# Message passing by one-hot matmuls: source chunks one-hot over 25 places instead of 50, two places packed into one number, and a reordered preparation

## The chip, the core and the metric

The kernel runs on one core of one Trainium2 chip. The metric is the device time of one execution in microseconds; lower is better. Engines are named as in the profile: PE (TensorE matmul) with PEld (its weight loads), DVE (VectorE), ACT (ScalarE), POOL (GpSimd) and SP (SyncE, which here only issues DMAs).

## What is computed

One layer of an edge convolution with 6250 nodes of 128 channels and 206250 edges (100000 random pairs in both directions and one loop per node), sorted by destination:

```python
h = jnp.maximum(_layernorm(x, axis=-1), 0.0)
# inside the layer, with src, dst of every edge
feat = jnp.concatenate([h[dst], h[src] - h[dst]], axis=-1)
msg = feat @ W.T + b
out = jax.ops.segment_max(msg, dst, num_segments=x.shape[0])
return x + jnp.where(jnp.isfinite(out), out, 0.0)
```

A message is a term that depends on the destination alone plus a row of a table `Bt` (6250 rows, one per source node). So the layer needs, for every destination, the maximum over its edges of the rows `Bt[src]`.

## The kernel before, in words

**Two ways to the same maximum.** The 6250 destinations are cut into 128 lanes of `LD = 49`. A source is written as place `l` of chunk `q`: 125 places, `Q = 50` chunks. For a destination and a chunk there is mostly at most one edge. This one goes the dense way: its place is found, turned into a one-hot column, and multiplied with the chunk of the table held in SBUF. A second edge in the same (destination, chunk) cell goes the sparse way: it is put on a list of its lane (`GR = 424` entries a lane, all lanes side by side), and the list is worked off row by row with indirect DMAs from `Bt` on POOL and a running maximum on DVE.

**Front (to about 145 us).** The edges of each lane are loaded (`WIN = 1792` wide), split into place (`vm`), chunk (`q16`) and destination in the lane (`dlc`). DVE compares the key with itself shifted by 1 to 41 places, PE adds the comparisons up in the PSUM tile `dup` (`shift`, L515), so that `dup` is zero for the first edge of each cell. `val` (L581) keeps `vm` for those alone. Eleven passes of masked copies (`pass_`, L615 and L616) then close up the listed entries in `pk`; spill over a lane's end is handed to the next lane through a DMA (`hand_over`, L653, into `first`). From `pk` come the indices `ridx` (L672) for the gathers. Beside the passes, and handed out to them in the lists `among` and `rest`, PE and ACT work off the list `micro`: for 25 pairs of chunks `turn` (transposes), `product` and `remainder`, which make the table and write it to DRAM by SP (L442). Also beside the passes, `turned` transposes `q16`, `dlc` and `val` into `TQ`, `TD`, `TV`, and `own_last` checks the loops. `make_sel` (L253) builds the selectors `Sel`.

**Main part (to about 750 us).** The lanes are cut into 13 tiles of 10 lanes (490 columns; the last has 8). A tile is cut into two units of 6 and 4 lanes. For a unit, `pieces` on DVE compares `TQ` with all 50 chunk numbers (`cmp_q`, four instructions, L754, into `OHQ`, 64 places per lane) and `TD` with 14 destinations (`cmp_d`, L758), and multiplies by `TV` (`mul_d`, L761). `mats` on PE then sums, for two lanes at a time, `OHQ` (the weights, 2 x 64 columns) with `OHD` (28 columns) into the PSUM tile `pv`, 14 blocks of edges each (L791): `pv[q, destination]` is the place. `square` on ACT (four instructions, L800 and L801) writes the place and its square to `Vb`. Then come 25 pairs of chunks, in each of which, for both chunks, `one_hots` makes `z = Sel.T @ Vb` (L859), ACT takes its Relu (L860), PE multiplies with two parts of the table into `ps` (L934, four matmuls), and DVE takes the maximum (L940). After each pair `more_rows` runs the sparse steps that are due: at pair k of 325 the list has to stand at `GR * (k - 2) // 310` rows, so the steps end 12 pairs before the last. A step is a min and max on DVE (`stream_step`, L152). Gathers (L82) are issued by POOL in groups of `U = 8` rows into a ring of `GB = 6` groups; group g is issued when the first step of group g - 5 has been issued. After each group SP writes its running maxima to the DRAM table `M` (L159), and the results at the ends of the runs are fetched by 49 more gathers from `M` into `R` (`get_rows`), two after each group, when they are due.

In tiles 1 and 2, ACT also counts ends of runs (L947), one instruction and its read of the accumulator after each pair. The order of everything is the order of the program on each engine; `at_pair` puts `mats`, `square`, `pieces` and the loads at given pairs, and `between` hands a piece to a pair that has two sparse steps, at the latest by a limit that falls from pair 6 to pair 11 of the unit.

**End.** The accumulated maxima are transposed, combined with `R` and with the destination's own term (L969 to L972), and written out (L974).

Of the kernel before, what the change touches and what calls it, by code (L numbers as in the profile page):

```python
# [19 lines left out]
P = 128  # L20
# [13 lines left out]
NS = 560  # L34
ST = 576
OV = 136
GR = 424
# [4 lines left out]
UL = 6  # L42
# [11 lines left out]
def gnn_kernel(tc, x, src, dst, W, b, out):  # L54
# [5 lines left out]
    KROW = 50  # L60
    GQ = 10
    NG = GR // U
    assert GR % U == 0 and NS == GR + OV and 2 * (WIN + OV) <= 1 << PB
# [24 lines left out]
    with ExitStack() as ctx:  # L88
# [13 lines left out]
        with ExitStack() as body:  # L102
# [7 lines left out]
            IQ = keep.tile([P, Q, NBLK], BF16, name="IQ")  # L110
# [5 lines left out]
            zero = keep.tile([P, 512], BF16, name="zero")  # L116
            ridx = keep.tile([P, GR], I32, name="ridx")
# [8 lines left out]
            shift_u = keep.tile([P, 1], F32, name="shift_u")  # L126
            shift_f = keep.tile([P, 1], F32, name="shift_f")
            over_ = keep.tile([P, 1], F32, name="over_")
# [10 lines left out]
            def gather_group():  # L139
                i = state["gathered"]  # L140
                state["gathered"] = i + 1
                for j in range(U):
                    k = i * U + j
                    gather(ring(i)[:, j], Bt[:, :], ridx[:, k:k + 1])

            def stream_step():
# [11 lines left out]
                if j == U - 1:  # L158
                    S_.dma_start(M_v[:, 1 + i * U:1 + i * U + U], G)  # L159

            with ExitStack() as pre:
# [47 lines left out]
                G_.affine_select(out=wrow, in_=wrow, compare_op=ALU.is_ge, fill=-2.0, base=SQ - 1,  # L209
                                 pattern=[[0, L + 1]], channel_multiplier=-1)  # L210
                G_.memset(wmask, 0.0)
                for step_, base in ((1, 0), (1, SQ)):
                    G_.affine_select(out=wmask, in_=wmask, compare_op=ALU.not_equal, fill=1.0, base=base,
                                     pattern=[[step_, Q]], channel_multiplier=-1)
# [13 lines left out]
                G_.memset(shift_u, float(L - MID))  # L228
                G_.memset(shift_f, L - MID + 0.5)
# [18 lines left out]
                for v in Vb:  # L248
                    V.memset(v, 0.0)
                    V.memset(v[32:64], 1.0)  # L250
# [72 lines left out]
                V.tensor_scalar_mul(negb, identb, -1.0)  # L323
                for r in range(2):
                    S_.dma_start(Bp[L:L + 1, r].bitcast(F32), at(frow, r * C, [list(frow.ap[0]), [0, Q], [1, C]]))
                S_.dma_start(M_v[:, 0], none)
                V.tensor_copy(IQ, row[:, 0, :Q].rearrange("p (q o) -> p q o", o=1).to_broadcast([P, Q, NBLK]))
# [103 lines left out]
                def remainder(k):  # L431
# [6 lines left out]
                    if o + 2 == GQ:  # L438
# [140 lines left out]
                keep_on(6)  # L579
                make_sel(30, 40)  # L580
                V.scalar_tensor_tensor(val, dup, 0.0, vm, op0=ALU.is_equal, op1=ALU.mult)  # L581
# [60 lines left out]
                for h in range(4):  # L642
                    rest[3 + h].append(lambda h=h: turned(q16, TQ, h))
                    rest[4 + h].append(lambda h=h: turned(dlc, TD, h))
                    rest[5 + h].append(lambda h=h: turned(val, TV, h))
                for i, j in ((6, 0), (7, 1), (8, 2), (8, 3)):
                    rest[i].append(lambda j=j: own_last(j))
                rest[8].append(lambda: A_.activation(junk[1], less, AF.Copy, accum_out=badc[:, 0:1]))
                for i in (7, 8, 9, 10):
                    rest[i].append(lambda: tick(8))  # L650
                def hand_over():
                    for p0, p1 in ((1, 113), (113, P)):
                        S_.dma_start(first[p0:p1], pk[p0 - 1:p1 - 1, GR:GR + OV])  # L653
# [11 lines left out]
                part = pk[:, :GR]  # L665
                V.tensor_scalar(lane_dl, tail_, DB, None, op0=ALU.logical_shift_right)
# [16 lines left out]
                make_sel(40, Q)  # L683
# [35 lines left out]
                V.memset(mend_i, 0)  # L719
# [4 lines left out]
            with ExitStack() as main:  # L724
# [12 lines left out]
                units = [(l0 + h, min(UL, l0 + nl - l0 - h)) for l0, nl in tiles for h in range(0, nl, UL)]  # L737
# [312 lines left out]
```

## Time and profile before

| | |
|---|---|
| time, median of 3 runs | 784.61 us (783.87 to 787.49) |
| the profiled execution | 782.91 us, of which its span is 781.1 us |
| mean granted TensorE clock | 0.948 |
| busy: PE, DVE | 646.3 us (83%), 718.3 us (92%) |
| busy: ACT, POOL | 484.0 us (62%), 491.7 us (63%) |

A row of a group in the profile reads: line, engine, operation, written tile <- read tiles, shapes (partitions x elements), count, then busy time in us and the mean duration of one in ns, then the idle time of the engine ahead of them and what ended it. A row of the timeline reads: start, duration (both us), engine, line, operation, count, and in brackets the idle time before it and what ended that. Durations on one engine overlap a little, since the next instruction starts before the last has drained. A view by stretches gives for each stretch the busy time of every engine and in brackets its number of instructions.

### The profile page before, as it was taken

The numbers are of one execution on the slowest core, as the hardware profiler recorded it, in microseconds if no ns is written. First come the engines' busy times: TensorE is split into PE (matmuls) and PEld (weight loads), VectorE is DVE, ScalarE is ACT, GpSimd is POOL, SyncE is SP. The second block draws the span as 40 slices with busy tenths as digits, with TensorE's granted clock in tenths as the row PEclk, the third lists the DMA queues.
The fourth block names the chain that finished last, engine by engine and source line by source line (L and its number), as shares of the span: only waits on it lengthen the run. The fifth ranks groups of instructions, "written<-read, shape, count | busy, mean of one in ns | idle before, by whom it ended". The sixth has DMA issues, their size and how long they took to land.

```text
span 781.1 us, 11909 instructions
## 1 busy us (share of the span) xinstructions
PE 646.3 (83%) x3623; PEld 464.5 (59%) x3630; DVE 718.3 (92%) x1290; ACT 484.0 (62%) x1035; POOL 491.7 (63%) x521
## 2 busy tenths in 40 slices
PE   0799867679898997989899898989998897887771
PEld 0455435467566765766666666667675565665660
DVE  6999899889999999899999999999998998887884
ACT  3655467336799997576666667575765556456430
POOL 4000000577777777777777777777777777777763
PEclk9999989869999998899999999999999999999995
DMA  6532144331533433343333434343343333333395
GB/s 194 132 99 75 25 100 108 106 91 52 145 107 104 117 105 92 108 114 105 105 97 97 114 105 115 105 118 105 102 115 92 105 103 96 100 105 108 98 235 183
DMA packets 83838, 85.50 MB, mean 109 GB/s; under 512 B 9954, under 2 KB 71640, under 8 KB 83512
## 3 DMA queue, kind: packets, MB, share of 16 engines
q1 hardware_dynamic: 67027, 47.62, 21.7%
q0 software_dynamic: 16176, 36.13, 17.0%
q10 hardware_dynamic: 564, 0.92, 0.4%
q8 instruction: 30, 0.49, 0.3%
q14 instruction: 41, 0.34, 0.1%
HBM read 46.96 MB, written 40.73 MB: 112 GB/s over the span
## 4 chain that ended last, share of the span: by engine, by line
DVE 26%; PE 16%; issue 14%; DMA 13%; ACT 6%; POOL 3%; POOLq 0%; DVEq 0%
DVE acc L940 16%; DMA X<-Bt,ridx 10%; PE ps L934 9%; DVE X L152 6%; PE z L859 4%; ACT oh L860 3%; DMA R<-M,last_e 3%; PE pv L791 3%; ACT counted L947 2%; POOL R L82 2%; DVE OHQ L754 1%; POOL X L82 1%; DVE acc L938 1%; DVE OHD L758 1%; DVE OHD L761 1%
## 5 line engine op out<-in xcount | busy, mean ns | idle before, releaser
L82 POOL DMA_INDIRECT X<-Bt,ridx x424 | 429.9, 1014 | 148.4 <-issue 42.0
L860 ACT ACTIVATE oh<-z 126x490 fp32r<-126x490 f32 (+1 forms) x650 | 338.3, 580 | 179.4 <-PE z L859 178.0
L934 PE MATMUL ps<-oh,Bp 126*128 126x490 f32 (+1 forms) x1300 | 396.9, 428 | 49.6 <-DVE acc L940 48.9
L940 DVE TENSOR_TENSOR acc<-acc,ps 128x980 f32<-128x980 f32 (+1 forms) x312 | 359.1, 1151 | 13.4 <-PE ps L934 11.6
L934 PEld LDWEIGHTS ps<-oh,Bp 126*128 126x128 f32 x1300 | 241.9, 195 | 150.0 <-DVE acc L940 104.0
L859 PE MATMUL z<-Vb,Sel 128*126 128x490 f16 (+1 forms) x650 | 197.0, 378 | 13.9 <-ACT oh L860 11.4
L152 DVE SCALAR_TENSOR_TENSOR X<-X,slim 128x128 f32<-128x128 f32 x423 | 145.6, 344 | 20.2 <-DMA X<-Bt,ridx 11.1
L859 PEld LDWEIGHTS <-Sel 128*126 128x126 f16 x650 | 87.1, 142 | 32.5 <-issue 4.2
L791 PEld LDWEIGHTS <-OHQ 128*128 128x128 bf16 x910 | 62.4, 162 | 17.7 <-issue 16.8
L791 PE MATMUL pv<-OHD,OHQ 128*128 128x28 bf16 (+1 forms) x896 | 67.1, 228 | 4.5 <-DVE OHD L761 4.4
L429 POOL DMA_DIRECT2D XA<-in_x x5 | 4.5, 901 | 105.2 <-DMA XA<-acc 105.2
L754 DVE TENSOR_TENSOR OHQ<-T,IQ 128x1092 bf16<-128x1092 bf16 (+5 forms) x104 | 61.6, 599 | 0.0
L82 POOL DMA_INDIRECT R<-M,last_e x49 | 48.4, 988 | 18.2 <-issue 9.4
L504 PE MATMUL dup<-T,identb 128*128 128x512 bf16 (+1 forms) x164 | 39.5, 363 | 1.7 <-DVE T L515 1.1
L947 ACT ACTIVATE counted<-lane_dl,nbias 128x560 bf16<-128x560 int32 x50 | 40.8, 815 | 0.1
L421 PE MATMUL pm<-wT,hT 128*125 128x256 f32 x100 | 30.8, 435 | 7.5 <-ACT hT L410 7.3
L421 PEld LDWEIGHTS pm<-wT,hT 128*125 128x125 f32 x100 | 19.9, 210 | 14.8 <-ACT hT L410 12.3
L504 PEld LDWEIGHTS <-identb 128*128 128x128 bf16 x168 | 16.1, 99 | 17.2 <-issue 4.5
L816 ACT COPY acc<-z 128x490 f32<-128x490 f32 (+1 forms) x13 | 7.3, 565 | 26.1 <-PE z L815 26.1
L616 DVE COPY_PREDICATED pk<-big,pk 128x1927 int32<-128x1927 int32 (+12 forms) x13 | 22.9, 1764 | 0.4
L404 ACT ACTIVATE hs<-X,nmr,rstd 125x128 f32<-125x128 f32 x50 | 22.1, 497 | 0.5 <-DVE nmr L301 0.5
L515 DVE TENSOR_TENSOR T<-KA,KB 128x1792 bf16<-128x1792 int16 x21 | 21.4, 1081 | 0.0
(255 smaller groups left out, 441.6 us busy)
## 6 DMA issues: line engine op xcount, KB each, us to landing
M<-X SPq DMA_DIRECT2D x53, 512.0 KB
X<-Bt,ridx POOLq DMA_INDIRECT x424
XA<-in_x POOLq DMA_DIRECT2D x5, 625.0 KB
ownb<-Bt SPq DMA_DIRECT2D x12, 245.0 KB
X<-in_x SPq DMA_DIRECT2D x5, 560.0 KB
Bt<-acc SPq DMA_DIRECT2D x5, 560.0 KB
XA<-acc SPq DMA_DIRECT2D x5, 560.0 KB
out_x<-R SPq DMA_DIRECT2D x10, 224.0 KB
```

Of the source, the lines that this page charges most:

```text
L82: G_.indirect_dma_start(out=o, out_offset=None, in_=table, in_offset=bass.IndirectOffsetOnAxis(ap=idx, axis=0))
L152: V.scalar_tensor_tensor(G[:, j], state["prev"], slim[:, k:k + 1], G[:, j], op0=ALU.min, op1=ALU.max)
L421: T_.matmul(pm[:L, j], hT[k % 2][:, j, :L], wT, start=False, stop=j == 1)
L504: T_.matmul(dup[:, c0:c1], w, e[:, c0:c1], start=first, stop=last)
L616: V.copy_predicated(pk[:, a:z], mask[:, a:z], pk[:, a + s:z + s])
L754: V.tensor_tensor(OHQ[:, :nl, a:z], over(TQ, z - a), iq, ALU.is_equal)
L791: T_.matmul(o, w, m, start=False, stop=True, skip_group_check=True)
L859: T_.matmul(z[:L + 1, :n], Sel[:, i + j], Vb[t % 2][:, :n], start=True, stop=True)
L860: A_.activation(oh[:, :n], z[:L + 1, :n], AF.Relu)
L934: T_.matmul(ps[:, j, :n], Bp[:, e, i + j], oh[j][:, :n], start=e == 0, stop=e == 1)
L940: V.tensor_tensor(a, a, ps[:, :, :n], ALU.max)
L947: A_.activation(counted.bitcast(BF16)[:, :NS], lane_dl, AF.Sign, scale=2.0, bias=nbias[:, c:c + 1], accum_out=ends[:, c:c + 1])
```

## The change

1. Chunk q of 25 to 49 shares a place in the one-hot with chunk q - 25. `OHQ` has 32 places a lane, of which 25 are compared (two `cmp_q` a unit instead of four), `mats` takes four lanes at a time (4 x 32 weight columns, 56 moving columns), and units are 4 and 6 lanes instead of 6 and 4. The place of an edge of an upper chunk is multiplied by 128 in the front (`upper`, `times`), so that `pv` holds lower place + 128 * upper place.
2. Per tile, `split` (two ACT instructions over the whole tile) rounds `pv / 128` to the upper place, `low` (one matmul with -128 on the diagonal) subtracts it from `pv`, and `features` (16 ACT instructions of 25 partitions, two or three lanes each) writes place and square of both halves to `Vb`. They are put at pairs 15 to 22 of the tile before; `square` was at pair 22. `mats` is put at pairs 0 and 2 of a unit instead of 2, 5 and 8.
3. In the front, `turn(k + 1)` comes ahead of `remainder(k)`. `val`, the transposes of `val`, `own_last` and `make_sel(30, 50)` come after `ridx`. Six filler matmuls ahead of `val` are gone. The second half of `hand_over` is issued by ACT, not SP. One gather from `M` into `mend` is put ahead of the first gathers, behind a memset on DVE.
4. `GR` is 420, not 424; the last group has four rows.

```diff
-NS = 560
+NS = 556
-GR = 424
+GR = 420
-UL = 6
+UL = 4
-    KROW = 50
+    KROW = 25
+    QH = Q // 2
+    HB = 32
+    DIG = 128.0
+    OFF = L - MID
...
-                micro = [f for k in range(NP_) for f in (lambda k=k: turn(k), lambda k=k: product(k),
-                                                         lambda k=k: remainder(k))]
+                micro = [lambda: turn(0)]
+                for k in range(NP_):
+                    micro.append(lambda k=k: product(k))
+                    if k + 1 < NP_:
+                        micro.append(lambda k=k: turn(k + 1))
+                    micro.append(lambda k=k: remainder(k))
...
-                keep_on(6)
-                make_sel(30, 40)
-                V.scalar_tensor_tensor(val, dup, 0.0, vm, op0=ALU.is_equal, op1=ALU.mult)
+                upper, times = junk
+                V.tensor_scalar(upper, q16, QH - 0.5, float(QH), op0=ALU.is_ge, op1=ALU.mult)
+                V.tensor_tensor(q16, q16, upper, ALU.subtract)
+                V.tensor_scalar(times, upper, (DIG - 1.0) / QH, 1.0, op0=ALU.mult, op1=ALU.add)
+                V.tensor_tensor(vm, vm, times, ALU.mult)
...
-                    rest[3 + h].append(lambda h=h: turned(q16, TQ, h))
-                    rest[4 + h].append(lambda h=h: turned(dlc, TD, h))
-                    rest[5 + h].append(lambda h=h: turned(val, TV, h))
-                for i, j in ((6, 0), (7, 1), (8, 2), (8, 3)):
-                    rest[i].append(lambda j=j: own_last(j))
-                rest[8].append(lambda: A_.activation(junk[1], less, AF.Copy, accum_out=badc[:, 0:1]))
+                    rest[6 + h].append(lambda h=h: turned(q16, TQ, h))
+                    rest[7 + h].append(lambda h=h: turned(dlc, TD, h))
...
-                    for p0, p1 in ((1, 113), (113, P)):
-                        S_.dma_start(first[p0:p1], pk[p0 - 1:p1 - 1, GR:GR + OV])
+                    for e, p0, p1 in ((S_, 1, 113), (A_, 113, P)):
+                        e.dma_start(first[p0:p1], pk[p0 - 1:p1 - 1, GR:GR + OV])
...
+                V.memset(mend_i, 0)
+                gather(mend, M[:P, :], mend_i[:, 0:1])
...
-                make_sel(40, Q)
+                V.scalar_tensor_tensor(val, dup, 0.0, vm, op0=ALU.is_equal, op1=ALU.mult)
+                for h in range(4):
+                    turned(val, TV, h)
+                for j in range(4):
+                    own_last(j)
+                A_.activation(junk[1], less, AF.Copy, accum_out=badc[:, 0:1])
+                make_sel(30, Q)
...
-                    ps = [lambda a=a, z=z: cmp_q(a, z) for a, z in ((0, 13), (13, 26), (26, 38), (38, Q))]
+                    ps = [lambda a=a, z=z: cmp_q(a, z) for a, z in ((0, 13), (13, QH))]
...
+                    z = min(a + 4, nl)
+                    for i in range(NBLK):
+                        w = OHQ[:, a:z, :, i].rearrange("p l q -> p (l q)")
+                        y = z - 1 if l0 + z == P else z
+                        todo = [(pv[:(z - a) * HB, off + a:off + y, near[i]:near[i] + WN], OHD[:, a:y, :, i])]
...
+                def split(t):
+                    n = cols[t]
+                    hi = two.tile([P, TL * LD], F32, name="hi", bufs=1)[:, :n]
+                    up = digits[t] = two.tile([P, TL * LD], BF16, name="up", bufs=1)
+                    A_.activation(hi, pvs[t][:, :n], AF.Identity, scale=1.0 / DIG, bias=magic[:, :1])
+                    A_.activation(up[:, :n], hi, AF.Identity, bias=magic[:, 1:])
+
+                def low(t):
+                    n = cols[t]
+                    T_.matmul(pvs[t][:, :n], ndig, digits[t][:, :n], start=False, stop=True, skip_group_check=True)
+
+                def features(t, h, j):
+                    n = cols[t]
+                    nl = n // LD
+                    src_ = (pvs[t], digits[t])[h][:, :n].rearrange("q (l d) -> q l d", d=LD)[HB * j:HB * j + QH, j:nl:4]
+                    v = Vb[t % 2][:, :n].rearrange("q (l d) -> q l d", d=LD)
+                    for k0, f, more in ((h * HB, AF.Copy, {}), (P // 2 + h * HB, AF.Square, {"bias": shift_f[HB * j:HB * j + QH]})):
+                        A_.activation(v[k0:k0 + QH, j:nl:4], src_, f, **more)
...
-                        for j, i in enumerate((2, 5, 8)):
-                            at_pair(p, i, lambda u_=p + 2, j=j: mats(u_, 2 * j, 2 * j + 2))
+                        for j, i in enumerate((0, 2)):
+                            at_pair(p, i, lambda u_=p + 2, j=j: mats(u_, 4 * j))
                         if p % 2:
-                            at_pair(p, 10, lambda t=(p + 2) // 2: square(t))
+                            t_ = (p + 2) // 2
+                            at_pair(p, 3, lambda t=t_: split(t))
+                            at_pair(p, 4, lambda t=t_: low(t))
+                            for k in range(8):
+                                at_pair(p, 4 + k - k // 4, lambda t=t_, k=k: features(t, 1 - k // 4, k % 4))
```

More of the change, by code (lines that the diff above doesn't have):

```diff
@@ L125, in gnn_kernel @@
             lane = keep.tile([P, 1], F32, name="lane")
-            shift_u = keep.tile([P, 1], F32, name="shift_u")
             shift_f = keep.tile([P, 1], F32, name="shift_f")
+            magic = keep.tile([P, 2], F32, name="magic")
             over_ = keep.tile([P, 1], F32, name="over_")
@@ L141, in gather_group @@
                 state["gathered"] = i + 1
-                for j in range(U):
+                for j in range(min(U, GR - i * U)):
                     k = i * U + j
@@ L803, in gnn_kernel @@
+                def square(t):
+                    split(t)
+                    low(t)
+                    for h in (1, 0):
+                        for j in range(4):
+                            features(t, h, j)
                 own_b = {}
@@ L844, in gnn_kernel @@
                         f()
-                    mats(u_, 0, UL)
+                    for a in (0, 4):
+                        mats(u_, a)
                 put_own(0)
```

72 lines of the change are left out of this document (34 added, 38 removed).

## The prediction

> **What bounds the kernel now.** I read the page's first parts, then the waits, then the groups, then stretches, and at last the timeline of POOL. The page's busy shares point at DVE, with its chain of work that ended last:
>
> ```profile
> PE 646.3 (83%) x3623; PEld 464.5 (59%) x3630; DVE 718.3 (92%) x1290; ACT 484.0 (62%) x1035; POOL 491.7 (63%) x521
> DVE 26%; PE 16%; issue 14%; DMA 13%; ACT 6%; POOL 3%; POOLq 0%; DVEq 0%
> L82 POOL DMA_INDIRECT X<-Bt,ridx x424 | 429.9, 1014 | 148.4 <-issue 42.0 <-DMA X<-Bt,ridx 39.6 <-DVE acc L940 21.0
> ```
>
> POOL's 63% misleads. The 148.4 us of idle time lie in slivers: from the first gather to the last, every gap is 0.30 us, whoever is named as its end. The timeline of POOL shows it (first gather, last gather, the first and the last fetch from M behind it; then the group of the fetches ahead of it):
>
> ```profile
> 143.82 1.37 POOL L82 DMA_INDIRECT X<-Bt,ridx  x1 [19.48 <-DVE swin L679]
> ...
> 735.69 0.95 POOL L82 DMA_INDIRECT X<-Bt,ridx  x1 [0.30 <-issue]
> 736.95 0.95 POOL L82 DMA_INDIRECT R<-M,last_e  x1 [0.30 <-issue]
> ...
> 770.51 0.94 POOL L82 DMA_INDIRECT R<-M,last_e  x1 [0.30 <-issue]
> ...
> L82 POOL DMA_INDIRECT R<-M,last_e x24 | 24.5, 1019 | 7.3 <-issue 4.3 <-DMA X<-Bt,ridx 3.0
> ```
>
> Between 143.82 and 736.64 POOL issues 424 gathers, 24 fetches, one gather of mend and one plain DMA: 450 in 592.8 us, 1.317 us each, never waiting. 25 fetches follow, and 9.6 us after the last of them the span ends. So POOL's queue is one unbroken chain from the front to the end, and the time is its start, plus the count of gathers, plus what lengthens one, plus the tail.
>
> DVE is a close second. In these stretches (columns: stretch, its length, busy us and instructions of PE, PEld, DVE, ACT, POOL, then clock, DMA) it is full from 440 to 580, and ACT is full in tiles 1 and 2:
>
> ```profile
> 213.00:260.00 47.00, 43.23 (x238) 32.09 (x237) 45.43 (x77) 45.35 (x107) 36.03 (x37) 0.96 0.36 101
> 260.00:306.00 46.00, 42.12 (x241) 31.49 (x239) 44.33 (x75) 44.27 (x104) 35.34 (x36) 0.96 0.41 114
> 440.00:580.00 140.00, 128.65 (x742) 95.24 (x741) 139.89 (x234) 91.42 (x177) 108.03 (x105) 1.00 0.39 109
> 580.00:736.00 156.00, 130.93 (x686) 96.84 (x684) 133.98 (x225) 89.46 (x178) 119.40 (x121) 0.95 0.36 101
> ```
>
> The groups up to 320 us say how far DVE's steps run behind the gathers: 133 against 105, 28 rows. After 580 DVE idles (133.98 of 156): it has caught up and waits for rows.
>
> ```profile
> L82 POOL DMA_INDIRECT X<-Bt,ridx x133 | 134.4, 1011 | 59.7 <-DVE swin L679 19.5 <-DMA X<-Bt,ridx 16.1 <-issue 12.8
> L152 DVE SCALAR_TENSOR_TENSOR X<-X,slim 128x128 f32<-128x128 f32 x105 | 36.1, 344 | 0.4
> ```
>
> **The change, part by part.**
>
> *Four rows fewer.* Four gathers at 1.317: -5.3 us on POOL's chain. Their four steps on DVE (0.34 each) lie beside it. The 49 fetches stay, and the tail with them: 0.
>
> *Half the comparisons.* The 104 comparisons of OHQ become 52. On DVE that is 30.8 us, off the path, since DVE isn't the bound. But a gather that meets them is longer:
>
> ```profile
> L754 DVE TENSOR_TENSOR OHQ<-T,IQ 128x1092 bf16<-128x1092 bf16 (+5 forms) x104 | 61.6, 599 | 0.0
> L761 DVE TENSOR_TENSOR OHD<-OHD,T 128x1176 bf16<-128x1176 bf16 (+2 forms) x26 | 17.0, 652 | 0.1
> L758 DVE TENSOR_TENSOR OHD<-T,IW 128x1176 bf16<-128x1176 bf16 (+2 forms) x26 | 16.9, 651 | 0.0
> ...
> 602.03 0.35 DVE L152 SCALAR_TENSOR_TENSOR X<-X,slim 128x128 f32<-128x128 f32 x1
> 602.30 0.72 DVE L754 TENSOR_TENSOR OHQ<-T,IQ 128x1092 bf16<-128x1092 bf16 x1
> 602.30 1.53 POOL L82 DMA_INDIRECT X<-Bt,ridx  x1 [0.30 <-DMA R<-M,last_e]
> ```
>
> An undisturbed gather takes 0.94; this one, begun together with a comparison, 1.53. The gathers' excess over 0.94 from the first to the last of the 474 rows of POOL is 32.9 us; 25.0 of it falls on the 154 gathers that overlap one of these three lines. By busy time 61.6 of 95.5 us is OHQ's: 16.1 us, of which half goes: -8.1. Bounds: 0 (the gather meets another DVE instruction instead) and -12 (the disturbance falls on OHQ alone). I take -8.1, in the middle, because the rows tie it to the length of the comparison. [...]
>
> *The start of POOL's chain.* The rows of the front around the removed instructions, and at its end:
>
> ```profile
> 88.41 1.46 DVE L253 TENSOR_TENSOR Sel<-wmask,wrow 128x1260 f16<-128x1260 f16 x1
> 91.69 0.38 PE L578 MATMUL pm<-ident,listed 128*1 128x128 f32 x2 [0.61 <-ACT T L574]
> 92.58 0.48 PE L418 MATMUL pm<-brow,bsel 128*125 128x512 f32 x1
> 92.90 1.02 PE L421 MATMUL pm<-wT,hT 128*125 128x256 f32 x4
> 92.94 2.02 DVE L581 SCALAR_TENSOR_TENSOR s<-dup,vm 128x1792 bf16<-128x1792 f32 x1 [3.06 <-PE dup L484]
> 94.88 0.27 DVE L582 TENSOR_SCALAR rows<-pm 1x128 f32<-1x128 f32 x1
> 96.02 0.43 PE L409 MATMUL pt<-ident,hs 125*128 125x125 f32 x2
> 96.51 0.14 DVE L590 COPY over__97<-pm 128x1 f32<-128x1 f32 x1
> ...
> 137.85 2.12 SPq L653 DMA_DIRECT2D first<-pk  x2
> 141.92 0.32 DVE L671 COPY_PREDICATED pk<-swin,first 128x136 int32<-128x136 int32 x1 [0.65 <-DMA first<-pk]
> 142.27 0.38 DVE L672 TENSOR_SCALAR ridx<-pk 128x424 int32<-128x424 int32 x1
> ```
>
> From 88.41 DVE now spends 1.46 on Sel, waits 3.06 for the filler matmuls and spends 2.02 on val. These leave; four passes over 1792 bf16 come in. Nearest rows are 0.63 for a pass with one input and 1.09 for one with two (below), so 3.4 us, done at 91.9. L582 then waits for L578, which ends at 92.07: it moves from 94.88 to 92.15, -2.7. L590, though, also waits behind PE's queue: the product (0.48 and 1.02) and the next turn (0.43) put it near 94.6 instead of 96.51: -1.9. At the end, `first` is there 4.1 us after its issue; its second half leaves SP, where the two issues take 2.12, and the earlier turn ends the table's DMAs before it: the wait of 0.65 goes. Sum -2.6. ACT's issue of the second half waits for the last pass with some transposes of dlc behind it; nothing before ridx needs them. The new gather into mend sits in POOL's 19.48 us of idle time; if its memset came late it would cost its 0.94, and if the first gather's 1.2 us behind ridx is a cold start, it takes that away. Bounds -4 and 0.
>
> ```profile
> L466 DVE TENSOR_SCALAR dlc__175<-d 128x1792 bf16<-128x1792 int16 x1 | 0.6, 629 | 0.0
> L473 DVE TENSOR_TENSOR KA<-T 128x1792 int16<-128x1792 int16 x1 | 1.1, 1093 | 0.0
> ```
>
> *ScalarE's part of split and features.* Four instructions of 0.467 (1.87 us a tile) become two over 490 columns and 16 over 147 or 98. The trace has no such shape; the nearest:
>
> ```profile
> L800 ACT ACTIVATE Vb<-pv,shift_u 50x245 f16<-50x245 f32 (+1 forms) x26 | 12.1, 467 | 0.4
> L816 ACT COPY acc<-z 128x490 f32<-128x490 f32 (+1 forms) x13 | 7.3, 565 | 26.1 <-PE z L815 26.1
> L295 ACT ACTIVATE rstd<-mv,eps 125x10 f32<-125x10 f32 x5 | 1.5, 306 | 3.6 <-DVE mv L291 3.6
> L437 ACT CAST Bp<-pm 125x256 fp32r<-125x256 f32 x25 | 9.5, 381 | 0.0
> ```
>
> Between 306 (10 columns) and 467 (245), both with a bias from memory, a Square of 147 or 98 takes about 0.40 or 0.37; from 381 for a plain copy of 256, a Copy about 0.30 or 0.27. Eight of each are 5.3, the split 2 x 0.6, together 6.5: +4.7 us a tile. Bounds: +3.3 (all at 0.25) and +7 (all at 0.467). Outside tiles 1 and 2 ACT is at 91.42 of 140, so this is covered. In tiles 1 and 2 it isn't: two tiles, +9.4 us on DVE's steps, which wait for the pairs. The first split and features, ahead of the loop, are bare too: +4.7. There DVE's moved val and longer Sel (2.0 and 1.5) add, and shorter pieces (four comparisons, 2.1), less PE work (28 matmuls) and the front's -2.6 take off: the loop starts about 4 us later measured from the first gather.
>
> What is late next is the ring: group g can't be gathered before the steps of group g - 5 have begun and its rows are written to M, so the steps may lag 40 rows, less two for that write. The lag of 28 grows by 4 + 9.4 us and by gathers 2.4 us faster by then, less the 2.4 us (four comparisons) that DVE saves in each of tiles 0 and 3: 11.0 us or some 9 rows. 37 of 38: I charge 2 us of waiting on POOL (0 to 8).
>
> *PE.* Its matmuls of L791 fall from 70 to 42 a tile, and one `low` is added; at 128.65 busy of 140 with DVE full, PE gains air and sets nothing. The earlier place of mats leaves at least one pair behind the last piece by the list's own limits. The rest of L791's gain is 0.
>
> *Sum:* -5.3 - 8.1 - 2.6 + 2 = -14.0 on the profiled execution's 782.9, so 768.9. That execution lies 1.7 under the median of the runs shown; against 784.61 it is 770.6.
>
> **The rivals.**
>
> (a) POOL never waits and the comparisons' share is the upper one: -5.3 - 12 - 3.5, about 764. For it: the lag after 580 is gone. Against: the ring's margin is one row.
>
> (b) The gathers stay at 1014 ns, since what lengthens them is not the comparison but whatever DVE runs beside it: -5.3 - 2.6 + 2 = -5.9, 778.7; if the ring costs 8 on top, no change (784). For it: gathers beside other DVE work carry 7.9 of the 32.9 us. Against it: 1.53 beside 0.94. [...]
>
> (c) Slower: ScalarE becomes the bound in pairs 15 to 22 of every tile. There it has eight pairs of Relu at 1.05, the split, 16 features and the copy of L816:
>
> ```profile
> 600.95 1.05 ACT L860 ACTIVATE oh<-z 126x490 fp32r<-126x490 f32 x2 [0.34 <-PE z L859]
> L940 DVE TENSOR_TENSOR acc<-acc,ps 128x980 f32<-128x980 f32 x132 | 153.8, 1165 | 0.0
> L938 DVE TENSOR_TENSOR acc<-ps,acc 128x980 f32<-128x980 f32 x6 | 7.0, 1170 | 0.0
> ```
>
> DVE's pair between 340 and 580 took 1.74 (240 us over 132 + 6 maxima) and would take 1.65, so eight are 13.2. ACT's are 8.4 + 6.5 + 0.57 = 15.5, and 2.3 too many; Relus run about one pair (1.7) ahead, so little is lost. With features at 0.467 and a split of 0.63 twice it is 17.7: 2.8 us lost in each of 10 tiles, and 2.2 more in tiles 1 and 2 and at the start, 35 in all. DVE has some 8 to spare: POOL needs 1.355 rows x 1.30 = 1.76 a pair and 24 fetches, so over the last 230 pairs DVE gains 25 + 31 us on its lag of 37 rows, 48 us. The end moves by 27, to 798. It decides from about 0.42 a feature. [...]
>
> **How the numbers follow.** Forecast 0.58 (own range 765 to 778), (a) 0.13, (b) 0.13, (c) 0.16. 0.5% is 3.9 us, about what a measurement of this kernel tells from no change. Faster: the forecast, (a) and 0.05 of (b): 0.76; same: the rest of (b), 0.08; slower: (c), 0.16. The range goes from 763 to 785, which leaves out most of (c) and the low end of (a).
>
> **What would show it.** In the profile after: the first gather near 141 instead of 143.82; POOL without gaps over 0.3 but for a few at groups between 300 and 400; the mean gather near 995 ns instead of 1014; OHQ x52; ACT full in tiles 1 and 2 and those tiles longer by some 5 us each; DVE with idle time in 440 to 580. It is wrong if POOL waits for DVE over long stretches, if gathers stay at 1014, or if ACT's features are 0.42 and over.

## The result, and the profile after

| | before | after |
|---|---|---|
| median | 786.08 us (6 runs) | 819.15 us (6 runs) |
| profiled execution's span | 781.1 us | 819.9 us |

The ratio is 1.041, 95% interval 1.035 to 1.046: 4% slower, against a forecast of 770.6 us and a range up to 785. The two profiled executions took 782.9 and 822.0 us, so their spans differ by 38.8 us where the medians differ by 33.1. Of the eighteen runs below, eleven fell on chips on which the kernel before took 1068 to 1103 us (medians), at a granted clock of 0.79 to 0.84 instead of about 0.95; such a run is called set aside, and no verdict rests on its time.

The groups of the changed kernel that answer to those quoted before:

```profile
L86 POOL DMA_INDIRECT X<-Bt,ridx x420 | 419.0, 998 | 156.4 <-issue 62.0 <-DVE X L158 35.4 <-DVE acc L986 17.4
L986 DVE TENSOR_TENSOR acc<-acc,ps 128x980 f32<-128x980 f32 (+1 forms) x312 | 360.3, 1155 | 74.5 <-PE ps L980 71.6 <-PE z L905 0.6
L906 ACT ACTIVATE oh<-z 126x490 fp32r<-126x490 f32 (+1 forms) x650 | 337.4, 577 | 158.9 <-PE z L905 157.1
L813 PE MATMUL pv<-OHD,OHQ 128*128 128x56 bf16 (+2 forms) x532 | 66.3, 285 | 11.8 <-DVE OHD L782 9.7 <-DMA ownb<-Bt 1.9
L775 DVE TENSOR_TENSOR OHQ<-T,IQ 128x728 bf16<-128x728 bf16 (+3 forms) x52 | 30.9, 600 | 0.0
```

The gather has come down to 998 ns (forecast 995), and DVE has lost 30.7 us of comparisons. But POOL now waits for DVE, and DVE for PE. The waits (engine and line that wait, what for, us in all, how often, the longest) of before:

```profile
DVE acc L940 <- PE ps L934: 11.6, 15, 1.6
...
PE z L859 <- ACT oh L860: 11.4, 22, 2.1
```

and of after:

```profile
DVE acc L986 <- PE ps L980: 71.6, 94, 3.5
...
PE z L905 <- ACT oh L906: 38.9, 79, 1.9
...
POOL X L86 <- DVE X L158: 35.4, 70, 6.7
```

Read from the bottom: POOL waits up to 6.7 us at a time for a sparse step, the step stands in DVE's queue behind a maximum, the maximum waits for PE's `ps`, and PE waits for ACT. By POOL's timeline the chain of gathers breaks in ten places between 269 and 465 us, 27.7 us beyond the ordinary gap of 0.30, and runs on unbroken from there. It no longer sets the time, the loop over pairs does. The chain of work that ended last, where ACT had 6% and DMA 13% before, says the same:

```profile
DVE 32%; ACT 28%; PE 24%; issue 12%; DMA 3%; POOL 1%; POOLq 0%; DVEq 0%; SPq 0%; ACTq 0%
```

The timeline of after shows the ends: first gather, first maximum (after 12.25 us of waiting), last gather, last combination of maxima.

```profile
142.12 1.06 POOL L86 DMA_INDIRECT X<-Bt,ridx  x1 [1.01 <-issue]
...
181.12 1.18 DVE L984 TENSOR_TENSOR acc<-ps,acc 128x980 f32<-128x980 f32 x1 [12.25 <-PE ps L980]
...
748.84 1.04 POOL L86 DMA_INDIRECT X<-Bt,ridx  x1 [0.31 <-DVE acc L986]
...
796.05 0.57 DVE L990 TENSOR_TENSOR acc<-acc 128x392 f32<-128x392 f32 x1
```

Before, the first maximum began at 170.48, the last gather ended at 736.64 and the last combination began at 751.64; now 46 us lie between these two, not 15. From the end of each tile's last combination (thirteen rows of L990, L944 before) come these stretches; the columns to the right are experiments that follow (`early_half` by its third run, `early_half_3`):

| us | before | after | `early_half` | `early_half_few` | `spread_front` | `b_half_cmp` |
|---|---|---|---|---|---|---|
| end of the first maximum | 171.7 | 182.3 | 180.5 | 177.6 | 177.5 | 173.7 |
| tile 0 from there | 42.9 | 46.5 | 43.4 | 42.9 | 42.9 | 41.8 |
| tiles 1 and 2 | 90.1 | 106.8 | 106.0 | 93.2 | 97.4 | 87.1 |
| tiles 3 to 8 | 266.0 | 293.4 | 283.8 | 274.3 | 281.1 | 263.5 |
| tiles 9 to 12 | 181.5 | 167.7 | 170.6 | 164.6 | 162.3 | 187.0 |
| from there to the end | 28.9 | 23.3 | 23.4 | 23.5 | 23.4 | 29.7 |
| span | 781.1 | 819.9 | 807.7 | 776.0 | 784.6 | 782.8 |

After minus before: +10.6 at the start, +3.6, +16.7 and +27.4 in tiles 0 to 8, together 58, then -13.8 where the kernel before had waited for gathers (DVE's steps 11.1 us in 11 waits), and -5.6 at the end. The stretches of after (columns as before: length, busy us of PE, PEld, DVE, ACT, POOL) for tiles 0, 1, 2 and the two long ones:

```profile
180.00:229.00 49.00, 43.09 (x201) 32.31 (x200) 38.83 (x53) 32.72 (x69) 37.73 (x39) 0.92 0.35 92
229.00:282.00 53.00, 41.96 (x197) 29.67 (x196) 41.67 (x68) 50.31 (x119) 38.68 (x39) 1.00 0.30 87
282.00:336.00 54.00, 45.68 (x205) 32.67 (x204) 42.69 (x69) 51.30 (x121) 32.79 (x34) 0.94 0.33 94
336.00:580.00 244.00, 211.78 (x996) 153.16 (x995) 212.01 (x359) 165.31 (x344) 175.97 (x178) 0.97 0.35 99
580.00:796.00 216.00, 192.99 (x927) 140.93 (x925) 195.18 (x315) 153.41 (x324) 145.18 (x147) 0.99 0.39 108
```

In tiles 1 and 2 ACT is full. From 336 on nobody is: DVE 212 of 244, PE 212, ACT 165. No engine's sum sets the time there; they take turns in waiting for each other. The ends of the maxima in DVE's timeline show where: on the mean of tiles 4 to 8 (43.5 us a tile before, 49.0 after), pairs 0 to 3 and 12 to 15, in which `mats` now stands, take 18.7 us instead of 13.6; pairs 16 to 22, with the features, 13.8 instead of 12.3; the other ten 16.5 instead of 17.6. Both places were tested.

### The profile page after: what moved, and what is told of

It reads as the page before. It is cut to its first block, busy times and chain, and to the rows that moved or that the text cites. A ratio compares the mean times of both kernels' runs of the same rounds, so it can differ in the third digit from the quotient of the medians.

```text
span 819.9 us, 11318 instructions
## 1 busy us (share of the span) xinstructions
PE 667.7 (81%) x3267; PEld 473.2 (58%) x3273; DVE 699.3 (85%) x1238; ACT 546.9 (67%) x1217; POOL 482.4 (59%) x523
## 4 chain that ended last, share of the span: by engine, by line
DVE 32%; ACT 28%; PE 24%; issue 12%; DMA 3%; POOL 1%; POOLq 0%; DVEq 0%; SPq 0%; ACTq 0%
ACT oh L906 13%; DVE acc L986 11%; PE ps L980 10%; ACT Vb L835 8%; PE pv L813 7%; PE z L905 5%; DVE X L158 4%; DVE T L531 4%; DVE pk L634 3%; ACT counted L993 2%; DVE big L633 1%; DVE stats L300 1%; ACT up L823 1%; ACT hi L822 1%; ACT acc L857 1%
## 5 line engine op out<-in xcount | busy, mean ns | idle before, releaser
L86 POOL DMA_INDIRECT X<-Bt,ridx x420 | 419.0, 998 | 156.4 <-issue 62.0
L980 PE MATMUL ps<-oh,Bp 126*128 126x490 f32 (+1 forms) x1300 | 398.1, 429 | 23.4 <-DVE acc L986 22.5
L905 PE MATMUL z<-Vb,Sel 128*126 128x490 f16 (+1 forms) x650 | 209.4, 377 | 48.4 <-ACT oh L906 38.9
L813 PE MATMUL pv<-OHD,OHQ 128*128 128x56 bf16 (+2 forms) x532 | 66.3, 285 | 11.8 <-DVE OHD L782 9.7
L813 PEld LDWEIGHTS <-OHQ 128*128 128x128 bf16 (+1 forms) x546 | 59.9, 164 | 23.2 <-issue 23.1
L86 POOL DMA_INDIRECT R<-M,last_e x49 | 47.5, 969 | 41.8 <-DMA M<-X 27.6
L993 ACT ACTIVATE counted<-lane_dl,nbias 128x556 bf16<-128x556 int32 x50 | 39.8, 796 | 0.3
L984 DVE TENSOR_TENSOR acc<-ps,acc 128x980 f32<-128x980 f32 (+1 forms) x13 | 15.1, 1163 | 21.1 <-PE ps L980 14.1
L775 DVE TENSOR_TENSOR OHQ<-T,IQ 128x728 bf16<-128x728 bf16 (+3 forms) x52 | 30.9, 600 | 0.0
L433 PE MATMUL pm<-wT,hT 128*125 128x256 f32 x100 | 28.6, 412 | 2.7 <-ACT hT L422 2.6
```

The lines of the kernel that those rows point to most:

```text
L86: G_.indirect_dma_start(out=o, out_offset=None, in_=table, in_offset=bass.IndirectOffsetOnAxis(ap=idx, axis=0))
L433: T_.matmul(pm[:L, j], hT[k % 2][:, j, :L], wT, start=False, stop=j == 1)
L813: T_.matmul(o, w, m, start=False, stop=True, skip_group_check=True)
L905: T_.matmul(z[:L + 1, :n], Sel[:, i + j], Vb[t % 2][:, :n], start=True, stop=True)
L980: T_.matmul(ps[:, j, :n], Bp[:, e, i + j], oh[j][:, :n], start=e == 0, stop=e == 1)
L993: A_.activation(counted.bitcast(BF16)[:, :NS], lane_dl, AF.Sign, scale=2.0, bias=nbias[:, c:c + 1], accum_out=ends[:, c:c + 1])
```

## The experiments

Theories: T1, the chain of gathers on POOL (the forecast's). T2, the bursts of `mats`, which stand right behind the last piece of the one-hots. T3, ACT's added instructions. T4, the front work that was moved behind the row numbers.

### Rows and comparisons, alone in the kernel before

`b_420` takes GR and NS of the change and nothing else.

```diff
-NS = 560
+NS = 556
-GR = 424
+GR = 420
```

> The kernel before, with parts of 420 rows instead of 424 and nothing else of the change (the last group of gathers and steps has four rows). All theories hold that the kernel before is bound by the chain of gathers on GpSimd, at 1.317 us a gather: 4 gathers less should give 4 to 6 us, a ratio of 0.993 to 0.995 to the kernel before. Were the pair loop on TensorE, ScalarE and VectorE as near to the bound already, as T2 and T3 make it after the change, it would be under 2 us.

782.09 us against 785.00, ratio 0.996 (0.993 to 0.999): 2.9 us (0.7 to 5.3). The 5.3 of the forecast lies at the edge of this; the direction is T1's. The mean gather of this profile is 1021 ns, with all comparisons in place, so means of single profiles differ by some ns.

`b_half_cmp` makes half the comparisons.

```diff
-ps = [... for a, z in ((0, 13), (13, 26), (26, 38), (38, Q))]
+ps = [... for a, z in ((0, 13), (13, 26))]
```

> The kernel before with the comparisons of q from 0 to 26 alone, two pieces for each unit instead of four (the other half of the one-hot stays zero, so the result lacks it); nothing else of the change. The forecast's term: a gather goes from 1014 to 995 ns, 8 us of 424 gathers, ratio 0.985 to 0.995. If the comparisons don't disturb the gathers: gathers stay at 1014 ns, ratio 0.998 to 1.002. If VectorE's saved 30 us matter beside that (T1 denies it, the loop before waited for GpSimd in its last tiles only): below 0.985.

783.19 us against 785.53, ratio 0.998 (0.994 to 1.001). Its gathers:

```profile
L82 POOL DMA_INDIRECT X<-Bt,ridx x424 | 430.3, 1015 | 147.4 <-issue 58.2 <-DMA X<-Bt,ridx 25.0 <-DVE acc L940 23.8
```

1015 ns against 1014, and 2.3 us in all (from 4.6 less to 0.5 more): the forecast's second term, -8.1 us, is not there, though a smaller one isn't excluded. Long gathers stay (by POOL's timelines between 200 and 700, 40 of 354 took over 1.2 us before, and 31 of 355 here, the longest 1.59 and 1.72 us). The excess over 0.94 us of the gathers and fetches that overlap a comparison of `OHQ` fell from 19.3 to 11.0 us, but that of all of them only from 32.9 to 32.2: nearly as much came back beside other work. Why gathers are 998 ns after the change stays open. The table shows what DVE's 30 us bought: tiles 0 to 8 are 6.6 us shorter, tiles 9 to 12 5.5 us longer. The loop ran ahead and then waited for POOL. So T1 holds for the kernel before, and of 30 us saved on DVE at most 4.6 show there.

### The bursts

`early_pieces` hands the pieces out by pair 7 instead of 11; `half_bursts` cuts each burst of 14 matmuls in two; `early_half` does both.

```diff
-for i in range(6, 12):
-    at_pair(p, i, lambda i=i: fill.update(most=11 - i))
+for i in range(3, 8):
+    at_pair(p, i, lambda i=i: fill.update(most=7 - i))
```
```diff
-for j, i in enumerate((0, 2)):
-    at_pair(p, i, lambda u_=p + 2, j=j: mats(u_, 4 * j))
+for j in range(4):   # mats(u_, first lane, first block, last block + 1)
+    at_pair(p, j, lambda u_=p + 2, j=j: mats(u_, j // 2 * 4, j % 2 * 7, j % 2 * 7 + 7))
```

> The changed kernel, with the pieces of the one-hots handed to VectorE at the latest by pairs 3 to 7 of each unit period instead of pairs 6 to 11, so that the last piece lies five pairs ahead of the matmuls that read it. T2 (the matmul bursts stand right behind the last piece, TensorE waits for it, and VectorE then waits for TensorE): the wait of L813 for OHD (9.7 us of VectorE in its worst row, and the 94 us that VectorE waits for L980) shrinks, tiles 4 to 8 go from 49 to 46 us each, and the whole to some 800 us (790 to 810). T3 (ScalarE's features are the cost): no change, 819. T1 (the gather chain on GpSimd sets the time): no change, 819. T4 (the front alone): no change.

> The changed kernel with each burst of 14 matmuls cut in two bursts of 7, at pairs 0, 1, 2 and 3 of a unit period instead of two bursts at pairs 0 and 2; the number and width of the matmuls stay. T2, in the form that it is the length of one burst that counts (1.65 us each, against 0.92 before the change): VectorE's wait for L980 behind a burst goes from up to 3.5 us to under 2, some 2 us a tile, 795 to 805 us in all. T2, in the form that the wait for the last piece counts: little change, since the first half still stands right behind that piece, 812 to 820. T3: no change, 819.

Both are set aside (1074 and 1065 us; so are `early_pieces` once more at 1077 and `early_half` twice at 1071 and 1082), so what each edit is worth alone stays open.

> The same kernel once more (pieces out by pair 7, bursts of 7 at pairs 0 to 3), because its two looks so far fell on chips that ran the kernel before in 1074 and 1081 us. On a chip that runs it in 785 us: T2 785 to 805 us with tiles 4 to 8 at 45 to 46 us; T3 815 to 820 us with tiles 4 to 8 at 49 us.

809.73 us, ratio 1.030 (1.024 to 1.036), against 1.041: about 8 us of the 33 come back, less than T2 asked. By the table it is 12.2 us of span: 1.8 at the start, 3.1 in tile 0, 0.8 in tiles 1 and 2, 9.6 in tiles 3 to 8, less 2.9 in tiles 9 to 12. In tiles 4 to 8 the pairs with bursts go from 18.7 to 16.5 us, still above the 13.6 of before. What a burst does, in the timeline of the changed kernel:

```profile
403.56 1.64 PE L813 MATMUL pv<-OHD,OHQ 128*128 128x56 bf16 x14 [1.14 <-DVE OHD L782]
...
405.51 1.05 ACT L906 ACTIVATE oh<-z 126x490 fp32r<-126x490 f32 x2 [3.08 <-PE z L905]
...
406.80 1.18 DVE L986 TENSOR_TENSOR acc<-acc,ps 128x980 f32<-128x980 f32 x1 [1.68 <-PE ps L980]
...
409.14 1.82 PE L813 MATMUL pv<-OHD,OHQ 128*64 128x28 bf16 x14
...
411.40 1.05 ACT L906 ACTIVATE oh<-z 126x490 fp32r<-126x490 f32 x2 [3.09 <-PE z L905]
...
412.45 1.18 DVE L986 TENSOR_TENSOR acc<-acc,ps 128x980 f32<-128x980 f32 x1 [1.77 <-PE ps L980]
```

PE waits 1.14 us for the last piece (L782, DVE), then holds the queue for 1.64; ACT starves 3.08 us, DVE 1.68. The second burst, with no wait ahead of it, does nearly the same. With both edits the longest wait of DVE falls from 3.5 to 2.1:

```profile
DVE acc L986 <- PE ps L980: 60.8, 100, 2.1
...
PE z L905 <- ACT oh L906: 39.0, 80, 1.9
```

PE's wait for ACT hasn't moved: that is another cause.

### What one matmul of a burst costs

`burst_kinds` gives the tiles four kinds of bursts.

```diff
+kind = t % 4
+m_ = OHD[:, a:y, :, i]              # kind 2: y = a + 2, two lanes only
+if kind == 1:
+    m_ = zero[:, :(y - a) * WN].rearrange("p (l w) -> p l w", w=WN)
+if kind == 3:
+    w = zero[:, :w.shape[1]]
-todo = [(pv[:(z - a) * HB, ...], OHD[:, a:y, :, i])]
+todo = [(pv[:w.shape[1], ...], m_)]
```

> A look at what one matmul of a burst costs. The changed kernel, but in tiles 1, 5 and 9 the moving operand is 56 columns side by side, all zero, in tiles 2, 6 and 10 only the first two lanes' 28 columns are moved against the same 128 weight columns, and in tiles 3, 7 and 11 the weights are 128 columns side by side, all zero (the one-hots' products are left out there); tiles 0, 4, 8 and 12 are unchanged. Unchanged: 0.118 us a matmul. If the number of matmuls sets the cost, as the prediction has it, all four kinds take 0.118. If the columns moved set it, tiles 2, 6 and 10 return to the 0.066 to 0.074 us of before; if their stride of 28 bytes does, tiles 1, 5 and 9 fall below 0.09; if the stride of the weights does, tiles 3, 7 and 11 do.

Its one execution took 803.20 us. The groups, with shapes apart (weights as partitions*columns, then moving partitions x columns; busy us over count is the cost of one in a burst):

```profile
L823 PE MATMUL pv<-OHD,OHQ 128*128 128x56 bf16 x98 | 11.7, 287 | 5.2 <-DVE OHD L782 5.2
L823 PE MATMUL pv<-OHD,OHQ 128*64 128x28 bf16 x84 | 10.9, 282 | 0.0
L823 PE MATMUL pv<-OHD,zero 128*128 128x56 bf16 x84 | 9.6, 281 | 1.2 <-DVE OHD L782 1.1
L823 PE MATMUL pv<-OHD,OHQ 128*128 128x28 bf16 x84 | 6.3, 228 | 1.1 <-DVE OHD L782 1.1
L823 PE MATMUL pv<-zero,OHQ 128*128 128x56 bf16 x84 | 6.2, 228 | 0.0
...
L823 PE MATMUL pv<-OHD,zero 128*64 128x28 bf16 x42 | 2.7, 231 | 0.0
```

For comparison, the kernel before by the same view:

```profile
L791 PE MATMUL pv<-OHD,OHQ 128*128 128x28 bf16 x882 | 65.3, 228 | 4.5 <-DVE OHD L761 4.4
```

0.119 us for 56 strided columns (0.114 with weights side by side), 0.074 for 56 side by side, 0.075 for 28 strided, as in the kernel before. So the columns and their stride of 28 bytes cost: if each of the 56 costs the same, an estimated 2.1 ns a column (0.119 / 56). For 28 that makes 0.060, and 0.075 was measured; what sets it there isn't shown. Two lanes alone are worse: 64 strided weight columns take 0.130, 64 side by side 0.064, while 128 strided ones show no such price (0.075 with 28 moving columns). Why 64 strided weight columns take longer than 128 isn't shown. Per tile the two kinds that the change uses make 28 x 0.119 + 14 x 0.130 = 5.15 us, against 70 x 0.074 = 5.2 before: 28 matmuls fewer, nothing saved.

`two_lanes` had two lanes a matmul (64 weight columns), in three bursts, with 8 feature instructions a tile.

```diff
-w = OHQ[:, a:z, :, i].rearrange("p l q -> p (l q)")
+w = OHQ[:, c:c + 2, :, i].rearrange("p l q -> p (l q)")   # for c in (a,), mats at pairs 0, 1, 2
```

> The changed kernel with two lanes a matmul instead of four: 28 moving columns and 64 weight columns, 70 matmuls a tile instead of 42, in bursts of 14 at pairs 0, 1 and 2; each feature instruction then covers five lanes, so there are 8 a tile instead of 16. If the four-lane matmul costs by its width (0.118 us against 0.066 us in the kernel before), TensorE does the same sum of work in shorter bursts (0.92 us against 1.65). T2: 800 to 810 us. T3: the features cost some 8 times 0.4 to 0.5, that is 3.6 us a tile instead of 5.3, a gain at the start and in tiles 1 and 2 of 4 to 5 us and a little in the others, 805 to 815. Were the number of matmuls the cost, as the prediction's 70 to 42 supposes, it would be slower than 819.

Both its runs, 1105 and 1092 us, are set aside. The second one's rows still show its weights, at a granted clock of 0.82:

```profile
L812 PE MATMUL pv<-OHD,OHQ 128*64 128x28 bf16 x882 | 117.1, 280 | 45.4 <-issue 31.5 <-DVE OHD L782 9.4 <-DVE OHQ L775 3.4
```

117.1 / 882 is 0.133 each, close to the 0.130 of `burst_kinds` and nearly twice what 128 weight columns cost there with the same 28 moving columns: the expectation, which went by the moving columns alone, was wrong.

### ScalarE's features

`few_features` leaves 12 of 16 feature instructions out of the changed kernel, `early_half_few` out of `early_half`.

```diff
-for j in range(4):            # ahead of the loop
+for j in range(1):
     features(t, h, j)
...
-for k in range(8):
+for k in (0, 4):
     at_pair(p, 4 + k - k // 4, lambda t=t_, k=k: features(t, 1 - k // 4, k % 4))
```

> The changed kernel without 12 of its 16 feature instructions a tile (only the first lane of each four gets its features, so the sums over the other lanes are left out of the result): ScalarE is relieved of some 4.0 us a tile (6 Copy of 0.27 to 0.31 and 6 Square of 0.36 to 0.40). T3 (ScalarE's added instructions are the cost): pairs 15 to 22 return to their times of before, the start is 4 us earlier, tiles 1 and 2 lose 8 us, 780 to 795 us in all. T2 (the bursts are the cost): only the start and tiles 1 and 2 gain, 805 to 812.

Both its runs, 1066 and 1064 us, are set aside.

> The kernel with early pieces and halved bursts (ratio 1.030 to the kernel before, some 810 us), without 12 of its 16 feature instructions a tile (the result lacks what they feed). T3 (ScalarE's added instructions are what is left): the first pair some 4 us earlier, tiles 1 and 2 some 5 to 8 us shorter each, pairs 15 to 24 of tiles 4 to 8 back from 20.2 to some 18 us: 775 to 788 us, ratio 0.985 to 1.005. T2 alone: only the bare start gains, 803 to 808 us, ratio 1.022 to 1.028. T1 would hold again if it came under 775 us: then the chain on GpSimd is once more what ends last.

777.66 us, ratio 0.989 (0.984 to 0.993): 32 us less than `early_half`, as T3 has it. By the table it is 2.8 at the start, 0.5 in tile 0, 12.8 in tiles 1 and 2, 9.5 in tiles 3 to 8, 6.0 in tiles 9 to 12; in tiles 4 to 8 the pairs 16 to 22 go from 13.7 to 12.5 us. The waits:

```profile
DVE acc L986 <- PE ps L980: 39.3, 64, 1.3
...
PE z L905 <- ACT oh L906: 6.2, 24, 0.9
```

PE's wait for ACT fell from 39.0 to 6.2. In the groups of the changed kernel, each of which mixes 147 and 98 columns, the features cost what was forecast (Square 0.40 or 0.37, Copy 0.30 or 0.27 us):

```profile
L835 ACT ACTIVATE Vb<-up,shift_f 25x98 f16<-25x98 bf16 (+1 forms) x52 | 20.6, 395 | 0.6
L835 ACT ACTIVATE Vb<-pv,shift_f 25x98 f16<-25x98 f32 (+1 forms) x52 | 18.5, 356 | 0.6
L835 ACT ACTIVATE Vb<-up 25x98 f16<-25x98 bf16 (+1 forms) x52 | 15.9, 305 | 1.2
L835 ACT ACTIVATE Vb<-pv 25x98 f16<-25x98 f32 (+1 forms) x52 | 13.9, 267 | 1.1
```

So their price was right. They stand close together, and right behind a burst. ACT in the changed kernel, from the split to the last features of a tile; the pairs in the middle hold two features each:

```profile
412.48 0.67 ACT L822 ACTIVATE hi<-pv,magic 128x490 f32<-128x490 f32 x1
...
416.10 1.06 ACT L906 ACTIVATE oh<-z 126x490 fp32r<-126x490 f32 x2
417.18 0.33 ACT L835 ACTIVATE Vb<-up 25x147 f16<-25x147 bf16 x1
417.52 0.42 ACT L835 ACTIVATE Vb<-up,shift_f 25x147 f16<-25x147 bf16 x1
417.96 1.05 ACT L906 ACTIVATE oh<-z 126x490 fp32r<-126x490 f32 x2
419.04 0.29 ACT L835 ACTIVATE Vb<-up 25x98 f16<-25x98 bf16 x1
419.34 0.38 ACT L835 ACTIVATE Vb<-up,shift_f 25x98 f16<-25x98 bf16 x1
419.74 1.05 ACT L906 ACTIVATE oh<-z 126x490 fp32r<-126x490 f32 x2
...
427.38 1.99 ACT L906 ACTIVATE oh<-z 126x490 fp32r<-126x490 f32 x4
```

There is no idle time in these 17 us, with 1.86 and 1.78 us from pair to pair, where the kernel before had a mean of 1.74. The four instructions of one pair (19), the split and the copy of L857 come on top. And ACT enters this stretch with nothing in stock: the row at 411.40 above, just ahead of the split, shows it starved for 3.09 us by the second burst.

### Place instead of amount, and the front

`spread_front` keeps the whole change. Features: one a pair at pairs 11 to 24. Counting: every other pair of tiles 1 to 4. Second unit's `mats`: pairs 6 to 9, pieces by pair 4, bursts halved, always 128 weight columns (two more zeroed lanes in `OHQ`). `val`, its `turned` and `own_last` are back ahead of `ridx`.

```diff
-at_pair(p, 4 + k - k // 4, lambda t=t_, k=k: features(t, 1 - k // 4, k % 4))
+at_pair(p, -1 + k * 14 // 16, lambda t=t_, k=k: features(t, 1 - k // 8, k // 2 % 4, (k % 2,)))
...
-if t in (1, 2):
+if 1 <= t <= 4 and i % 4 == 0 and c < LD + 1:
```

> The whole change with its work placed otherwise: features one instruction a pair at pairs 11 to 24 instead of four a pair at pairs 16 to 22, the fifty counting instructions at every other pair of tiles 1 to 4 instead of every pair of tiles 1 and 2, the second unit's matmuls at pairs 6 to 9 with their pieces out by pair 4, bursts halved and always 128 weight columns wide, and the added front work (val, its turning, own_last) back ahead of the row numbers as in the kernel before. If T3 is a matter of place (ScalarE is full only in pairs 16 to 22 and in tiles 1 and 2: 0.67 to 0.70 us a feature pair and 1.15 us of Relu against some 1.75 us a pair): tiles 1 and 2 at 46 to 47 us, tiles 4 to 8 at 45, the first pair near 178 us, 775 to 788 us, ratio 0.985 to 1.003. If it is their sum: 795 to 810 us, ratio 1.012 to 1.030.

788.12 us, ratio 1.002 (1.000 to 1.005): all but 2 of the 33 us are back, with every instruction of the change kept. The waits:

```profile
DVE acc L988 <- PE ps L982: 40.2, 67, 1.7
...
PE z L907 <- ACT oh L908: 24.6, 41, 1.1
```

Mostly place, then: against `early_half` this placing gives 22 us with all features there, where leaving most of them out gave 32; the other 10 stay open. It moves features, counting, bursts and front at once, so the share of the features' place alone isn't shown. And the change, placed this way, only draws level. The front's part, by the profiled executions: the first gather comes at 143.63 here, and at 140.62 to 142.12 in the four kernels above that have this work behind `ridx` (the changed kernel, `early_half_3`, `burst_kinds`, `early_half_few`); the first `z` comes at 171.40 here, and at 174.35 to 175.51 in the first three of these, which have all features. The moved work buys GpSimd some 1.5 to 3 us and costs the pair loop 3 to 4. `front_back` (that part alone) and `spread` (all but that part) were to settle T4:

> The changed kernel with only the moved front work put back as in the kernel before: val, its turning and own_last ahead of the row numbers, the turning of q16 and dlc three passes earlier, ten columns of the selection table back ahead of the sort. T4 (this work behind the row numbers delays the pair loop, which is the bound): the first pair at some 178 us instead of 182.3, the first gather perhaps 1 to 2 us later than 142.1, in all 3 to 6 us less than 819, ratio 1.033 to 1.037. If GpSimd's chain were the bound (T1): 1 to 2 us more than 819, with the first gather.

> The kernel with features and counting spread out, the second unit's matmuls at pairs 6 to 9, bursts halved and 128 weight columns wide, but the front as the change has it (so spread_front without the front's part). If the front is worth 3 to 6 us in the pair loop: 791 to 795 us, ratio 1.006 to 1.011. If the front is worth nothing once the loop is relieved: as spread_front, 788 us, ratio 1.002.

Both are set aside (1103 and 1082 us), so T4 rests on those profiles, and what it is worth in the whole stays open.

`b_front` is `b_420` with the earlier turns and the hand-over on two queues.

```diff
...
-                for p0, p1 in ((1, 113), (113, P)):
-                    S_.dma_start(first[p0:p1], pk[p0 - 1:p1 - 1, GR:GR + OV])
+                for e, p0, p1 in ((S_, 1, 113), (A_, 113, P)):
+                    e.dma_start(first[p0:p1], pk[p0 - 1:p1 - 1, GR:GR + OV])
```

> The kernel before with parts of 420 rows, each turn of the front ahead of the remainder before it, and the hand-over of the first rows on two queues. By the forecast's terms: 4 to 6 us for the rows (2.9 measured) and 2.6 us for the front (0 to 4), so 776 to 781 us, ratio 0.988 to 0.995. If the front's reordering brings nothing by itself: as with the 420 rows alone, ratio 0.996.

780.27 us against 786.15, ratio 0.991 (0.988 to 0.994): a little under 1% faster than the kernel before, and the fastest here that computes the whole result. Against the 0.996 of `b_420` the intervals just overlap, and its first gather isn't earlier in the profiled execution:

```profile
144.34 1.36 POOL L82 DMA_INDIRECT X<-Bt,ridx  x1 [23.61 <-DVE swin L683]
```

144.34 against 143.82. So what the reordering adds to the rows isn't shown.

## Why the prediction was wrong

The path was wrong: the time was summed on POOL's chain of gathers, and the loop over pairs became the path instead. The steps that let this happen are ACT's added work "covered" outside tiles 1 and 2, and PE, which "gains air and sets nothing". Term by term:

- **Four rows, -5.3:** 2.9 measured, with an interval that reaches 5.3. Right in kind.
- **Half the comparisons, -8.1:** wrong. Alone it moves the gather by 1 ns and the whole by 2.3 us (at most 4.6). One row with 1.53 beside 0.94, and a share by busy time, were read as a cause; the excess beside comparisons did fall with them, but nearly as much came back beside other work. The rival (b), under which the gathers stay, was right for the comparisons by themselves. That the gather came down to 998 ns in the whole change is, as far as this run shows, luck.
- **Start of POOL's chain, -2.6:** 143.82 to 142.12, -1.7. But the reordered turns show no gain by themselves; the work moved behind `ridx` gives it, and it comes back in the loop.
- **The loop starts 4 us later, measured from the first gather:** 12.3 later (39.0 us from the first gather to the first maximum, for 26.7). `val`, its transposes and `own_last` were costed as DVE's time alone; DVE also stands 2.8 us in one wait for PE, whose queue they fill. This and the split and features of the first tiles, which lie ahead of the loop with nothing beside them, were taken to be absorbed by the ring, because the loop wasn't thought to be the bound.
- **Tiles 1 and 2, +9.4:** 16.7 measured. ACT full was right (50.3 us busy of 53), and without most features the two tiles fall from 106.0 to 93.2. Why a full ACT costs more here than its own excess isn't shown.
- **ACT covered outside tiles 1 and 2:** this is the step that failed first. Its price was right: split and features take 6.7 us a tile, for 6.5. The overlap was wrong: without 12 of 16 features, tiles 3 to 12 are 15.5 us shorter (`early_half_few` against `early_half`). The step compared sums over a stretch (91 busy of 140). The features stand in seven pairs of 25, and there ACT takes 1.8 us and more a pair. Rival (c) named the place, but let it decide only from 0.42 us a feature, by a sum over eight pairs with a stock of one pair of Relus ahead and 8 us of spare time in DVE; at a mean of 0.33 us it decided already, and in the tile shown the burst ahead had used up the stock.
- **PE "gains air and sets nothing":** this failed too. It gained nothing, L813 66.3 us for 67.1, as the wide matmul costs 1.6 times the narrow one. And the "at least one pair behind the last piece" was not there: PE runs ahead of DVE, so it stood 1.14 us waiting for a piece that DVE had yet to make. Earlier pieces and halved bursts together are worth 8 us.
- **The ring, +2:** 27.7 us of gaps beyond the ordinary ones. The first stand in tiles 1 and 2, where the margin of one row was eaten. They followed from the late loop and didn't set the end: the last gather came 46 us before the last combination.

The sum was made on one engine's chain, and every other term was measured against whether it lengthened that chain. The loop was charged 4 + 9.4 us, which the ring was to take. It lost 58 us up to tile 8; 19 of these fell on time in which it had waited before (-13.8 and -5.6), and the rest is the 39 us by which the profiled span grew.

## What to carry to other kernels

Where two chains run within a few per cent of each other, cost a change on both, and compare an engine's load with the pace pair by pair, not by its share over a stretch: here, instructions that fit on the average (ACT busy 165 of 244 us) stalled the loop where they were bunched, and placing features, counting, bursts and front otherwise gave back 31 of 33 us. The matmul count said little here, with strided operands (42 a tile took 5.15 us, 70 had taken 5.2); take the cost of one burst from the trace, by columns. Before booking a gain to an overlap seen in a few rows, halve the suspected work alone.

## What the runs showed of the hardware, unexpected

56 moving columns 28 bytes apart cost 0.119 us a matmul (an estimated 2.1 ns a column, 0.119 / 56), 56 side by side 0.074; 64 strided weight columns cost 0.130 us a matmul, 128 strided ones 0.075 with the same 28 moving columns. Half the comparisons on DVE left the mean indirect DMA issue on POOL at 1015 ns, for 1014, although issues beside a comparison were among the longest (1.53 us at 602.30 in the kernel before, whose longest gather between 200 and 700 us took 1.59).
